# A fused two-layer graph network with a mixture of experts: the dispatch's triangle product a step later for full chunks, the router's product behind the second values for the first 16 batches

## The chip, the cores and the metric

The kernel runs on one core of one Trainium2 chip. Its time is device time in microseconds (us), as a median of several runs. A core has five engines that work in parallel, each with its own queue of instructions: TensorE (PE) for matmuls, VectorE (DVE) and ScalarE (ACT) for elementwise work, GpSimd (POOL), and SyncE (SP), which here only issues DMAs. POOL issues DMAs too, those that are addressed through a list of row numbers (indirect ones). In the profile PEld is TensorE's loading of weights, which runs beside its matmuls.

## The reference

The input `x` is 64 batches of 256 rows by 256 columns in float32, with one 256 x 256 adjacency matrix for all. Two layers follow each other, and each has an attention over the graph and a feed-forward part, both behind a layer norm and with a residual:

```python
x = x + _L0_gnn_ref(_layernorm(x), adj, L0_gnn_W, L0_gnn_a)        # 4 heads of 64, elu
x = x + _L0_ffn_ref(_layernorm(x), L0_ffn_weight, L0_ffn_bias)     # one linear
x = x + _L1_gnn_ref(_layernorm(x), adj, L1_gnn_W, L1_gnn_a)        # 1 head of 256, relu
x = x + _L1_ffn_ref(_layernorm(x), router_w, w1, b1, w2, b2)       # 8 experts, top 2

# the expert part, for tokens = the normed rows
probs = jax.nn.softmax(logits, axis=-1)
rw, re = jax.lax.top_k(probs, 2)
rw = rw / jnp.maximum(rw.sum(-1, keepdims=True), 1e-12)
out = tokens
for e in range(8):
    h = jax.nn.gelu(tokens @ w1[e] + b1[e], approximate=False)
    out = out + combine[:, e:e + 1] * (h @ w2[e] + b2[e])
```

`combine` holds a token's two weights at its two experts and zero elsewhere. Because `out` starts at the tokens, the last layer's output is the residual, plus the normed rows, plus what the experts add.

## The kernel before

Each batch's 256 rows are two tiles of 128 (NT = 2). `batch_layers` computes all of a batch up to its router logits. 62 batches then send each row to its two experts (dispatch), and the last two are computed with all experts (dense). The 62 go in chunks: 12 of four batches, six of two, two of one (`CHUNKS`). I call the 12 full chunks; in the code they are those with `spread`.

**How the order is made.** The whole order of work is written by the kernel itself. Each batch, each chunk's `route` and each expert pair is a Python generator, and the main loop (L1091 onwards) goes through time in steps. In a step every active generator is resumed once, in order of its rank, smallest first, and emits instructions until its next `yield r`, which sets its rank for the next step; a negative rank puts it back into the same step. Every engine gets its instructions in the order in which they are emitted. A batch takes three steps to the next (`TICKS`), so steps have phases 0, 1 and 2; a new batch begins in phase 2. `later(rank, *phases)` yields until a step of one of the phases comes. About five batches are under way at a time, each in another part of `batch_layers`.

**A batch.** The rows' mean and variance come from DVE (`norm_stats`: stats L374, mv L375), and POOL makes rstd of them (`finish_norms`: L382, L383). In most steps two norms meet, and one POOL pair of 128x4 serves both (`half_done` holds the first until the second comes). A norm that stays alone is finished at the end of the step, as 128x2. Then: layer 0's projections pq (L405), q scaled on DVE (L421), scores pd (L475) and z (L482), values pv (L496, 128x65), rinv (L503), the linear pf (L560) with x (L566, DVE, with rstd), layer 1's pq (L440), scores pd and z (L459, L464), values pv (L496, 128x257), their sum into x (L586), a last norm with `by` (L591, L594), the normed rows `xng` and the output's base (ACT, L600, L605), a transpose (pt L389, copied to xT by ACT, L395), and the router's product pl (L630), whose copy is the logits `lg` (L634). Of the ranks near the change: pl has 35, in phase 2, and the second values (pv 128x257) have 40, in the same step.

**A chunk's dispatch.** `route` begins in the step of its last pl. `top_two` gives one-hots of the two best experts and ends with their sum `m` (L948, all on DVE). Two products `pp` with a triangle of minus ones and with ones (PE, L956 and L957) count the rows of each expert; `both`, a running sum and a second addition (DVE, L959 to L975) make positions, `pos` (L978 to L985) picks each row's two, `ed` is an exponential on ACT (L961), `two_weights` (DVE, L679 to L682) makes the two weights, and the last copies (L989) put them beside the rows. In a full chunk these parts lie in steps of phase 2 (`m`), 0 (pp to L975), 2 (pos), 0 (weights, copies). Then POOL sends the rows (L922, an indirect DMA for each tile and expert, two a step, rank 95).

**Expert pairs.** A pair is 256 rows of one expert. SP loads its rows (xr, xt) once the chunk's sends have landed, DVE transposes them (sT), PE computes ph (L816) and py (L831), ACT the gelu between them (hT, L822), DVE adds the bias (y, L841), ACT multiplies by the weight (L809), and `scatter` (L852, rank 97, two indirect DMAs on POOL) adds the result to the output rows in DRAM. Pairs of different experts can meet in a row, so each scatter waits until those of the pair before it have landed.

In the last steps, the drain, no new batches come; norms then stay alone more often, and only pairs are left in the end.

Of the kernel before, what the change touches and what calls it, by code (L numbers as in the profile page):

```python
# [11 lines left out]
AF = mybir.ActivationFunctionType  # L12
# [15 lines left out]
def kernel(  # L28
# [17 lines left out]
    nc = tc.nc  # L46
# [5 lines left out]
    NT = N // P  # L52
# [307 lines left out]
    half_done = []  # L360
# [19 lines left out]
    def finish_norms(n):  # L380
        mv, rstd = half_done.pop()
        nc.gpsimd.tensor_scalar_add(rstd[:, :n], mv[:, :n, 1], EPS)  # L382
        nc.gpsimd.tensor_tensor(rstd[:, :n], rstd[:, :n], mhalf[:, :n], ALU.pow)  # L383

    def transposed(src, tag="xT", bufs=4, blocks=False):
        pt = bank("pt", [KT, N])
        for t in range(NT):
            for k in range(KT):
                nc.tensor.transpose(  # L389
                    pt[:, k, t * P : (t + 1) * P],  # L390
                    by_block(src[:, t, :])[:, k] if blocks else src[:, t, k * P : (k + 1) * P],
                    ident,
                )
        dst = work.tile([P, KT, N], F32, tag=tag, name="xT", bufs=bufs)
        nc.scalar.copy(dst, pt)  # L395
        return dst
# [109 lines left out]
    def batch_layers(b, c0, xng, lg):  # L506
# [23 lines left out]
        early = b < EARLY  # L530
# [92 lines left out]
            based.append(d.ins)  # L623
            nc.sync.nop()
        xT = transposed(xe[:, :, :D], *(("xTd", DENSE) if dense else ()), blocks=True)
        yield 35
        pl = bank("pl", [NT, E])
        for t in range(NT):
            for k in range(KT):
# [47 lines left out]
    def two_weights(less, second, ed):  # L677

        nc.vector.tensor_scalar(less, ed, 1.0, None, op0=ALU.add)  # L679
        nc.vector.reciprocal(less, less)  # L680
        nc.vector.tensor_tensor(second, ed, less, ALU.mult)
        nc.vector.tensor_tensor(less, less, second, ALU.subtract)  # L682
# [250 lines left out]
    def later(rank, *phases):  # L933

        yield rank
        while more and order_steps[-1] % TICKS not in phases:
            yield rank

    def route(c, row0, nt, n, last, xng, lg):

        rt = lambda shape, name, bufs=2, dt=F32: chunk_tile(shape, name, c, bufs, dt)
        vec, tt = nc.vector, nc.vector.tensor_tensor
        yield -90

        tail = rt([nt, 3], "tail")
        ohs, ed = top_two(c, nt, lg, tail[:, :, 0])
        m = rt([E, nt], "m")
        tt(m.rearrange("p e t -> p t e"), ohs[:, 0], ohs[:, 1], ALU.add)  # L948


        spread = nt == NTC
        yield from later(90, *((0,) if spread else (1, 2)))

        mf = m.rearrange("p e t -> p (e t)")
        pp = bank("pp", [2, E, nt])
        nc.tensor.matmul(pp[:, 0].rearrange("p e t -> p (e t)"), tri, mf, start=True, stop=True)  # L956
        nc.tensor.matmul(pp[:, 1].rearrange("p e t -> p (e t)"), ones, mf, start=True, stop=True)  # L957
        both = rt([2, E, nt], "both")
        vec.tensor_copy(both, pp)  # L959
        pre, tot = both[:, 0], both[:, 1]  # L960
        nc.scalar.activation(ed, ed, AF.Exp)  # L961
        tt(tot[:, :, 0], tot[:, :, 0], rows[0], ALU.add)
        run = rt([E, nt], "run")
        if nt == NTC:
            vec.tensor_tensor_scan(
                run.rearrange("p e t -> p (e t)"), scan_mask.rearrange("p e t -> p (e t)"),
                tot.rearrange("p e t -> p (e t)"), 0.0, ALU.mult, ALU.add,
            )
        else:
            for e in range(E):  # L970
                vec.tensor_tensor_scan(
                    run[:, e, :], ones[:, :nt], tot[:, e, :], 0.0, ALU.mult, ALU.add
                )
        rows[0] = run[:, :, nt - 1]
        tt(pre, pre, run, ALU.add)  # L975
        if spread:
            yield from later(90, 2)
        tt(  # L978
            ohs, ohs, pre.rearrange("p e t -> p t e")[:, None].to_broadcast([P, 2, nt, E]),
            ALU.mult,  # L980
        )
        posf = rt([2, nt], "posf")
        vec.tensor_reduce(posf, ohs, AX.X, ALU.add)
        pos = rt([2, nt], "pos", 4, I32)
        vec.tensor_copy(pos, posf)  # L985
        yield from later(90, *((0,) if spread else (1, 2)))
        two_weights(tail[:, :, 1], tail[:, :, 2], ed)
        for i, xe in enumerate(xng):
            vec.tensor_copy(xe[:, :, D + 1 :], tail[:, i * NT : (i + 1) * NT, :])  # L989
        parts = allot(c, n, False)  # L990
        if n and not spread:
            next(parts)
            ids, ef = next(parts)
        if last:
            ends_at = rt([E], "ends_at", 2, I32)
            vec.tensor_copy(ends_at, rows[0])
        yield 95
        mark = len(sent)
        for t in range(nt):
            for k in range(2):  # L1000
                send(xng[t // NT][:, t % NT, :], pos[:, k, t : t + 1])
            if n and spread and t in (1, 4):
                ids, ef = next(parts) or (None, None)
            if not last:
                yield 95
            elif t % 2:
                yield 95
        needs = sent[mark:]
        if n:
            regs = {}  # L1010
            waiting.extend(
                lambda j=j: expert_pair(j, n, ids, ef, regs, needs) for j in range(n)
            )
        if last:
            parts = allot(c + 1, FLUSH, True)
            next(parts)
            ids2, ef2 = next(parts)
            _, ends_sp = nc.values_load_multi_w_load_instructions(
                ends_at[0:1, :], engines=[mybir.EngineType.SP], min_val=0,
                max_val=(E * CAP - 1) * PAIR, skip_runtime_bounds_check_because="rows of a region",  # L1020
            )
            filled = []
            for e in range(E):
                d = nc.sync.dma_start(
                    out=xs_d[bass.ds(ends_sp[e], PAIR), :].rearrange("(p t) c -> p t c", t=2),
                    in_=fill,
                )
                tc.declare_no_dep(
                    d.ins, query=SYNC, group="rows", reason="filling rows lie behind an expert's last row"
                )  # L1030
                tc.add_to_no_dep_group("rows", d.ins)
                filled.append(d.ins.name)
                nc.sync.nop()
            yield 95
            regs2 = {}
            waiting.extend(
                lambda j=j: expert_pair(j, FLUSH, ids2, ef2, regs2, filled)
                for j in range(FLUSH)
            )
# [50 lines left out]
    with tc.manual_schedule():  # L1090
        while more or active or waiting or dense_jobs or scatters:  # L1091
            phase = step % TICKS
            if phase == 2 and more:
                nxt = next(batches, None)
                more = nxt is not None
                if more:
                    begin(nxt, 25)
            if step >= SETUP_AT and setup:
                begin(setup.pop(0)(), 90)
            if step >= QUIET:  # L1100
                if waiting and len(scatters) < 3:
                    begin(waiting.pop(0)(), 90)
            elif phase == 1:
                credit = min(credit + 3.0, 2.0 if step < DRAIN_AT else 3.0)
                while waiting and credit >= 1.0:
                    credit -= 1.0
                    begin(waiting.pop(0)(), 90)
            if dense_jobs and step % DENSE == 0:
                begin(dense_jobs.pop(0)(), 90)
            if scatters:  # L1110
                def one():
                    scatter()
                    return
                    yield
                begin(one(), 97)
            order_steps.append(step)
            queue = [(a[0], a[1], a) for a in active]
            heapq.heapify(queue)
            while queue:
                *_, entry = heapq.heappop(queue)  # L1120
                entry[0] = next(entry[2], None)
                if entry[0] is not None and entry[0] < 0:
                    entry[0] = -entry[0]
                    heapq.heappush(queue, (entry[0], entry[1], entry))
            if half_done:
                finish_norms(NT)
            active[:] = [a for a in active if a[0] is not None]
            step += 1
# [35 lines left out]
```

The softmax here doesn't subtract the row's maximum and nothing guards it: scores larger than these inputs give would overflow.

## Time and profile before

| what | value |
|---|---|
| median of 3 runs | 1607.51 us (1606.32 to 1608.09) |
| profiled execution | 1611.36 us, of which 1609.5 us is the span of the profile |
| PE busy | 1468.2 us (91%) |
| PE weight loads busy | 1299.9 us (81%) |
| DVE busy | 1308.6 us (81%) |
| POOL busy | 914.6 us (57%) |
| ACT busy | 860.2 us (53%) |
| mean granted PE clock | 0.963 |
| rows L831 py and L816 ph, PE | 266.5 and 243.6 us |
| row L496 pv, PE | 370.3 us |
| row L852 scatter, POOL | 417.0 us, 262 of 1592 ns |
| row L922 send, POOL | 251.2 us, 248 of 1013 ns |

The span in 40 equal slices of about 40 us, each digit the busy share in tenths, PEclk the clock that was granted to PE:

```profile
PE   7998988999999999999999999999999999489960
DVE  6898988999898989898989899899899987545530
POOL 2332636265757576666657575756665567733444
PEclk9999998999999999999999999999999999799985
```

The setup and the first batches fill the first slices. From the ninth slice on PE is full to within a tenth. In the 35th the last batches leave the pipeline, and after the 38th PE has next to nothing to do. A busy PE is not PE at its peak: matmuls are pipelined and their ends are modelled.

### The profile page before, as it was taken

How to read it: one execution, taken by the hardware profiler on the slowest of the kernel's cores; microseconds unless marked ns; L12 is line 12 of the kernel's file. 1: busy time of each engine (PE TensorE's matmuls, PEld its weight loads, DVE VectorE, ACT ScalarE, POOL GpSimd, SP SyncE). 2: the span in 40 equal slices, each digit the busy share in tenths (PEclk: the TensorE clock that was granted, in tenths of full speed). 3: DMA queues.
4: the chain of work that ended last, by engine and by line, in shares of the span. 5: the costliest groups of instructions: out<-in, count | busy, mean ns of one | idle time of the engine just before them, and what ended most of it. 6: DMA issues, size and time to landing. Idle time of an engine off the chain costs nothing.

```text
span 1609.5 us, 30304 instructions
## 1 busy us (share of the span) xinstructions
PE 1468.2 (91%) x8474; PEld 1299.9 (81%) x8474; DVE 1308.6 (81%) x4431; ACT 860.2 (53%) x1968; POOL 914.6 (57%) x875
## 2 busy tenths in 40 slices
PE   7998988999999999999999999999999999489960
PEld 5887777888888888888888888888888887468850
DVE  6898988999898989898989899899899987545530
ACT  2455455465666666556666665555556655343320
POOL 2332636265757576666657575756665567733444
PEclk9999998999999999999999999999999999799985
DMA  5712223466666666665657576664766566787733
GB/s 156 207 50 57 83 74 90 113 152 131 134 145 135 141 143 133 149 145 126 156 119 152 130 155 126 159 129 108 155 129 152 131 120 134 185 174 152 133 47 45
DMA packets 364134, 207.39 MB, mean 129 GB/s; under 512 B 264248, under 2 KB 334912, under 8 KB 363968
## 3 DMA queue, kind: packets, MB, share of 16 engines
q1 hardware_dynamic: 313344, 137.07, 34.7%
q0 software_dynamic: 49632, 67.39, 23.0%
q8 instruction: 70, 1.15, 0.3%
q10 hardware_dynamic: 992, 0.99, 0.2%
q14 instruction: 96, 0.79, 0.2%
HBM read 116.19 MB, written 89.15 MB: 128 GB/s over the span
## 4 chain that ended last, share of the span: by engine, by line
PE 70%; DVE 17%; DMA 3%; ACT 3%; issue 3%; POOL 2%; SPq 1%; DVEq 0%; POOLq 0%; ACTq 0%
PE pv L496 16%; PE ph L816 14%; PE py L831 14%; PE pq L405 6%; PE pq L440 6%; PE pf L560 5%; PE pt L389 4%; DVE z L482 3%; DVE stats L374 2%; PE pl L630 2%; ACT xT L395 2%; DMA out_dram<-y,xt 2%; POOL out_dram L852 1%; DVE mv L375 1%; PE pd L475 1%
## 5 line engine op out<-in xcount | busy, mean ns | idle before, releaser
L852 POOL DMA_INDIRECT out_dram<-y,xt x262 | 417.0, 1592 | 199.7 <-issue 51.1
L496 PE MATMUL pv<-q,z 128*128 128x65 f32 (+1 forms) x2560 | 370.3, 300 | 1.3 <-DVE z L482 1.3
L496 PEld LDWEIGHTS pv<-q,z 128*128 128x128 f32 x2560 | 331.5, 194 | 13.8 <-DVE z L482 1.4
L922 POOL DMA_INDIRECT xs<-xng,pos x248 | 251.2, 1013 | 66.4 <-issue 63.7
L382 POOL TENSOR_SCALAR rstd<-mv 128x4 f32<-128x4 f32 (+1 forms) x132 | 59.3, 449 | 395.5 <-DVE mv L375 347.5
L831 PE MATMUL py<-w2s,hT 128*128 (+1 forms) x1176 | 266.5, 380 | 1.2 <-ACT hT L822 1.2
L395 ACT COPY xT<-pt 128x512 f32<-128x512 f32 x192 | 113.7, 592 | 276.3 <-PE pt L389 276.3
L816 PE MATMUL ph<-sT,we 128*128 128x256 f32 x1048 | 243.6, 386 | 10.0 <-DMA we<-wpack 7.8
L831 PEld LDWEIGHTS py<-w2s,hT 128*128 128x128 f32 x1176 | 219.9, 191 | 30.0 <-ACT hT L822 2.0
L816 PEld LDWEIGHTS ph<-sT,we 128*128 128x128 f32 x1048 | 199.2, 194 | 37.2 <-issue 8.2
L482 DVE SCALAR_TENSOR_TENSOR z<-pd,q,mask 128x256 f32<-128x256 f32 x512 | 211.1, 474 | 0.9 <-PE pd L475 0.9
L822 ACT ACTIVATE hT<-ph,we 128x256 f32<-128x256 f32 x294 | 122.4, 472 | 152.9 <-PE ph L816 130.9
L383 POOL TENSOR_TENSOR rstd<-rstd,mhalf 128x4 f32<-128x4 f32 (+1 forms) x132 | 162.7, 1233 | 11.0
L374 DVE BATCH_NORM_STATS2 stats<-x 128x6 f32<-128x256 f32 x384 | 156.2, 407 | 2.2
L809 ACT ACTIVATE y<-y,w 128x256 f32<-128x256 f32 x262 | 112.4, 501 | 76.0 <-DVE y L841 75.5
L440 PE MATMUL pq<-wx,xT 128*128 128x259 f32 x512 | 130.1, 397 | 18.6 <-ACT xT L395 14.9
L405 PE MATMUL pq<-wx,xT 128*128 128x268 f32 x512 | 133.9, 407 | 5.6 <-DVE xT L116 3.7
L841 DVE TENSOR_TENSOR y<-py,b2s 128x512 f32<-128x512 f32 x131 | 85.9, 685 | 57.9 <-PE py L831 52.6
L440 PEld LDWEIGHTS pq<-wx,xT 128*128 128x128 f32 x512 | 92.5, 190 | 45.2 <-ACT xT L395 29.7
L560 PE MATMUL pf<-wfT,xT 128*128 128x256 f32 x512 | 122.8, 383 | 0.1
L405 PEld LDWEIGHTS pq<-wx,xT 128*128 128x128 f32 x512 | 99.0, 198 | 25.1 <-issue 3.2
L375 DVE BATCH_NORM_AGGREGATE mv<-stats 128x2 f32<-128x6 f32 x512 | 93.1, 182 | 17.5
(156 smaller groups left out, 2262.3 us busy)
## 6 DMA issues: line engine op xcount, KB each, us to landing
we<-wpack SPq DMA_DIRECT2D x139, 288.0 KB
xr<-xs SPq DMA_DIRECT2D x524, 64.0 KB
xblk<-in_x_dram SPq DMA_DIRECT2D x256, 64.0 KB
xin<-in_x_dram SPq DMA_DIRECT2D x64, 256.0 KB
out_dram<-base SPq DMA_DIRECT2D x64, 256.0 KB
out_dram<-y,xt POOLq DMA_INDIRECT x262, 4.1
xs<-xng,pos POOLq DMA_INDIRECT x248, 2.7
xs<-fill SPq DMA_DIRECT2D x9, 260.0 KB
```

The costliest lines, as they stand in the source:

```text
L374: nc.vector.bn_stats(stats[:, t, :], src[:, t, :])
L383: nc.gpsimd.tensor_tensor(rstd[:, :n], rstd[:, :n], mhalf[:, :n], ALU.pow)
L395: nc.scalar.copy(dst, pt)
L405: nc.tensor.matmul(pq.rearrange("p h c -> p (h c)"), xT[:, k, t * P : (t + 1) * P], wx[:, k, :], start=(k == 0), stop=(k == KT - 1),)
L440: nc.tensor.matmul(pq, xT[:, k, t * P : (t + 1) * P], wx1[:, k, :], start=(k == 0), stop=(k == KT - 1),)
L482: nc.vector.scalar_tensor_tensor(z[:, j, :], pd[:, i, :], q[:, j, h, d + 2 : d + 3], mask[:, j, :], op0=ALU.max, op1=ALU.mult,)
L496: nc.tensor.matmul(pv[:, h, :], z[:, j, t * P : (t + 1) * P], q[:, j, h, : d + 1], start=(j == 0), stop=(j == NT - 1),)
L560: nc.tensor.matmul(pf[:, t, :], xT[:, k, t * P : (t + 1) * P], wfT[:, k, :], start=(k == 0), stop=(k == KT - 1),)
L816: nc.tensor.matmul(ph[:, f, :], we[:, k * D + f * P : k * D + (f + 1) * P], xT[:, k, :], start=(k == 0), stop=(k == KT - 1),)
L831: nc.tensor.matmul(py[:, t, :], hT[:, f, t * P : (t + 1) * P], w2s[:, e, f * D : (f + 1) * D].rearrange("p e c -> p (e c)"), start=(f == 0 ...
L852: d = nc.gpsimd.indirect_dma_start(out=out_rows, out_offset=bass.IndirectOffsetOnAxis(ap=xt[:, t, 0:1].bitcast(I32), axis=0), in_=y[:, t, ...
L922: d = nc.gpsimd.indirect_dma_start(out=xs_d[: E * CAP * PAIR, :], out_offset=bass.IndirectOffsetOnAxis(ap=at, axis=0), in_=xe, in_offset=None,
```

## The change

Four things are edited.

- `batch_layers`: for the first 16 batches (`early`) the router's product pl gets rank 45 instead of 35, which puts it behind the second values (rank 40) in the same step.
- `route`, full chunks: the products pp, with the exponential of `ed`, move from the step of phase 0, rank 90, to that of phase 1, rank 45. The DVE work on them (both, the running sum, the addition) and `two_weights` follow in the step after, of phase 2, and pos with the last copies in the one after that, of phase 0. The sends stay in the step where they were.
- `route`, the eight smaller chunks: the steps of pp, pos and the copies stay; `two_weights` comes in the step of pp, in front of pos, instead of in the step of the copies.
- The main loop: before an entry of a rank above 75 is resumed, a norm that is still alone is finished, so its two POOL instructions stand ahead of that step's sends and scatters. Before, they stood at the end of the step.

```diff
--- before.py
+++ after.py
@@ -623,7 +623,7 @@
             based.append(d.ins)
             nc.sync.nop()
         xT = transposed(xe[:, :, :D], *(("xTd", DENSE) if dense else ()), blocks=True)
-        yield 35
+        yield 45 if early else 35
         pl = bank("pl", [NT, E])
         for t in range(NT):
             for k in range(KT):
@@ -949,16 +949,21 @@
 
 
         spread = nt == NTC
-        yield from later(90, *((0,) if spread else (1, 2)))
+        if spread:
+            yield from later(45, 1)
+        else:
+            yield from later(90, 1, 2)
 
         mf = m.rearrange("p e t -> p (e t)")
         pp = bank("pp", [2, E, nt])
         nc.tensor.matmul(pp[:, 0].rearrange("p e t -> p (e t)"), tri, mf, start=True, stop=True)
         nc.tensor.matmul(pp[:, 1].rearrange("p e t -> p (e t)"), ones, mf, start=True, stop=True)
+        nc.scalar.activation(ed, ed, AF.Exp)
+        if spread:
+            yield 90
         both = rt([2, E, nt], "both")
         vec.tensor_copy(both, pp)
         pre, tot = both[:, 0], both[:, 1]
-        nc.scalar.activation(ed, ed, AF.Exp)
         tt(tot[:, :, 0], tot[:, :, 0], rows[0], ALU.add)
         run = rt([E, nt], "run")
         if nt == NTC:
@@ -973,8 +978,9 @@
                 )
         rows[0] = run[:, :, nt - 1]
         tt(pre, pre, run, ALU.add)
+        two_weights(tail[:, :, 1], tail[:, :, 2], ed)
         if spread:
-            yield from later(90, 2)
+            yield 90
         tt(
             ohs, ohs, pre.rearrange("p e t -> p t e")[:, None].to_broadcast([P, 2, nt, E]),
             ALU.mult,
@@ -983,8 +989,8 @@
         vec.tensor_reduce(posf, ohs, AX.X, ALU.add)
         pos = rt([2, nt], "pos", 4, I32)
         vec.tensor_copy(pos, posf)
-        yield from later(90, *((0,) if spread else (1, 2)))
-        two_weights(tail[:, :, 1], tail[:, :, 2], ed)
+        if not spread:
+            yield from later(90, 1, 2)
         for i, xe in enumerate(xng):
             vec.tensor_copy(xe[:, :, D + 1 :], tail[:, i * NT : (i + 1) * NT, :])
         parts = allot(c, n, False)
@@ -1118,6 +1124,8 @@
             heapq.heapify(queue)
             while queue:
                 *_, entry = heapq.heappop(queue)
+                if half_done and entry[0] > 75:
+                    finish_norms(NT)
                 entry[0] = next(entry[2], None)
                 if entry[0] is not None and entry[0] < 0:
                     entry[0] = -entry[0]
```

No instruction is added or taken away. In the instruction order of the two kernels POOL's differs in four places, all in the drain, and SP's in none.

## Prediction

> **What bounds the kernel now.** I read the windows by stage first, then PE's and DVE's waits, then the timelines where a wait stood, and the chain of waits for the end. Every window starts with its stretch and length, then the busy time of PE, PEld, DVE, ACT and POOL, PE's granted clock, DMA share and GB/s:
>
> ```profile
> 145.00:200.00 55.00, 49.87 (x312) 43.67 (x311) 50.59 (x165) 27.36 (x80) 28.88 (x33) 0.97 0.24 73
> 330.00:700.00 370.00, 365.71 (x2191) 327.24 (x2190) 333.17 (x1101) 224.28 (x487) 244.28 (x228) 1.00 0.65 141
> 1310.00:1415.00 105.00, 80.55 (x393) 69.06 (x392) 69.98 (x325) 53.76 (x113) 73.61 (x68) 0.87 0.71 152
> 1550.00:1609.00 59.00, 4.06 (x19) 3.23 (x17) 1.38 (x2) 3.25 (x8) 25.50 (x17) 0.58 0.36 44
> ```
>
> There are three regimes. Up to about 314 us PE and DVE are equally full (49.87 and 50.59 of 55). From 330 to about 1284 PE is full (365.71 of 370). In the drain no engine is full, and after 1550 only POOL's scatters are left. PE's waits over the whole run:
>
> ```profile
> PE pp L956 <- DVE m L948: 19.8, 4, 11.3
> PE pl L630 <- ACT xT L395: 8.2, 7, 2.3
> PE pt L389 <- ACT xng L600: 8.0, 1, 8.0
> ```
>
> The four pp waits are 2.74 us at 134.91, 3.72 at 206.03, 2.05 at 281.22 and 11.26 at 1378.36. The first three (8.5 together) are full chunks in the early regime; the fourth is a small chunk in the drain. DVE in the drain:
>
> ```profile
> DVE by L591 <- POOL rstd L383: 18.1, 3, 10.1
> DVE x L566 <- POOL rstd L383: 9.0, 2, 6.4
> ```
>
> So the drain's long waits all come from rstd, made on POOL. POOL's timeline shows why (start, duration, work):
>
> ```profile
> 1337.75 1.02 POOL L922 DMA_INDIRECT xs<-xng,pos  x1 [0.18 <-issue]
> 1339.07 1.00 POOL L922 DMA_INDIRECT xs<-xng,pos  x1 [0.30 <-issue]
> 1340.42 1.61 POOL L852 DMA_INDIRECT out_dram<-y,xt  x1 [0.35 <-issue]
> 1342.34 1.57 POOL L852 DMA_INDIRECT out_dram<-y,xt  x1 [0.30 <-ACT hT L822]
> 1343.38 0.82 POOL L382 TENSOR_SCALAR rstd<-mv 128x2 f32<-128x2 f32 x1
> 1344.28 0.73 POOL L383 TENSOR_TENSOR rstd<-rstd,mhalf 128x2 f32<-128x2 f32 x1
> ```
>
> and DVE's on both sides of it:
>
> ```profile
> 1329.20 0.18 DVE L375 BATCH_NORM_AGGREGATE mv<-stats 128x2 f32<-128x6 f32 x1
> ...
> 1338.49 0.18 DVE L375 BATCH_NORM_AGGREGATE mv<-stats 128x2 f32<-128x6 f32 x1
> 1345.05 0.88 DVE L566 SCALAR_TENSOR_TENSOR x<-pf,rstd,x1b 128x256 f32<-128x256 f32 x2 [6.38 <-POOL rstd L383]
> ```
>
> The mv that this rstd reads was finished at 1329.38; the rstd stood behind two sends and a scatter pair, and DVE idled 6.38 us. The end itself is a chain of scatters (chain of waits):
>
> ```profile
> 1560.30 1.54 POOL out_dram L852
> 1561.84 0.30 issue
> 1562.14 3.77 DMA out_dram<-y,xt
> 1566.04 0.71 issue
> 1566.75 1.54 POOL out_dram L852
> ```
>
> A pair of scatters starts about 0.84 us after the pair before it has landed, at least 6.45 us a pair. I number the 131 pairs from 0. From pair 88 (1284.35) to pair 130 (1599.71) nearly all start so; what they lose beyond 0.84 us in the drain is POOL's norms and sends between two pairs: pair 93 4.71, pair 96 0.84, pair 100 2.26, pair 102 0.89, pair 103 1.52, and little else. y never holds them: the last y (ACT L809) is done at 1555.4, its scatter starts at 1599.7; pair 108's y is done by 1426.6 and goes at 1445.1. So only what moves this chain in the drain, or its start by way of PE, moves the end.
>
> **What the Trainium skill says.** "Perfetto Trace Analysis", Tensor Engine Instruction: ACT, DVE and GpSimd queues are strict FIFO, PE alone pulls weight loads ahead. The trace agrees: an rstd with its data ready since 1329.38 stood until 1343.38. "DMA: Bandwidth & Descriptors", Rules for kernel authors: an accumulating DMA needs the earlier DMA's semaphore before it touches the same bytes; that is the chain above, 0.84 us after each landing. "TensorE: Matmul & The Clock Gate", What's actually happening: after an idle window of about 3.4 us PE drops to half clock. The trace agrees: after the wait of 3.72 us eight pq matmuls (L405) took 3.89 us, where such a group takes 1.97 at full clock.
>
> **The change part by part.** No instruction is added or removed; PE, DVE, ACT and POOL only have theirs in another order. SP's order is the same, and POOL's differs in four places.
>
> *1. pp a step later for the 12 full chunks.* The one-hots (top_two and m, about 3.1 us of DVE) end at 205.88 in the second chunk; the products then stood in front of PE's pq at 206.03. Now PE meets them a step later, with m long ready: the three early waits go. But DVE was busy through them and does the same work after. What DVE loses to PE there is little: rinv waits 1.60 at 142.85 and 1.60 at 214.83, z (L464) 0.82 at 211.33. These go. In return both, add, scan, add (0.26+0.17+0.29+0.22, about 1.0 with gaps) leave the step where they filled DVE's wait for the norm chain (mv, POOL 1.34, ACT 0.44); in steps without them q (L421) waits 1.0 to 1.1. Chunk by chunk: -1.6+1.1, -1.6-0.8+1.1, and 0+1.0 for the third: -0.8. Bounds: all of DVE's early waits on PE (3.5 rinv, 0.8 z, 0.5 x between 100 and 314 us) gone and no new one, -4.8; no gain and three new waits, +3.3. At 313.8 PE takes over, waiting 1.82 for by, so DVE's time is what carries. I take -0.8.
>
> *2. pl behind pv for 16 batches.* PE's 7.9 us of early waits for xT lie where DVE sets the pace; pv comes earlier by pl's 0.96 us, lg (L634) later by pv's 1.98, and top_two follows on a DVE that is behind. 0; it lies within the bounds of part 1.
>
> *3. The nine full chunks after 330 us.* PE does the same work and is full, its waits there 16 us in all, none of them pp. both, add, scan, add and two_weights (1.0+0.75) come into phase 2 where pos (0.85) was: +0.9 us of DVE at that step's end, as much less in others. The same place takes the 3.1 us of top_two a batch earlier without PE waiting, so 0.9 is covered: 0. Uncovered it would be 12 x 0.9 = +10.8. The bank of pp is held one step longer, its next use lies 16 allocations on: 0. In the eight small chunks two_weights precedes pos: z 0.75 us later, under 24 ph matmuls (5.2 us): 0. Exp of ed moves by a step or less on an ACT that is 53% busy; its table loads stay 106: 0.
>
> *4. A single rstd ahead of everything of rank above 75.* On POOL this moves four norms, all in the drain: ahead of the sends and pair 92, of the sends and pair 95, of the sends and pair 99, and from behind pair 102 to before it. A single norm costs 1.0 alone and 1.6 behind a scatter. Queued behind it are two sends (1.3 each) and the pair.
> - Pair 92: the norm's mv is ready (1310.25), the sends start 1.1 later; the pair +1.0. Its rstd is there at 1313.6, so x (L566) is bound by its own place on DVE, 1317.4 instead of 1319.97; the pair norm that follows and was waited for (mv at 1321.92) runs 2.6 earlier; pair 93 -2.7 and pair 94 -2.8 (1331.1).
> - Pair 95: IOTA, norm, two sends from 1334.0: 1338.8, -1.6. Its rstd is done at 1336.0, and L566 now starts when DVE is through its earlier work, 1338.67+0.75 = 1339.4, not 1345.05. The next pair norm is done by 1343.7; pair 96 is bound by landing, 1346.1: -2.5. Pairs 97 and 98 keep this.
> - Pair 99: norm and sends end at 1367.5, landing asks for 1367.8: -2.5. by (L591) comes at about 1365 instead of 1374.85. Pair 100: four sends without the norm (1.8) before them, 1376.8: -3.4. Pair 101 the same.
> - Pair 102: POOL had 4.67 idle in front of it, so the norm is free there: -3.4. Pair 103: four sends, no norm: 1400.6, against 1404.99: -4.4.
>
> From pair 104 on landing bounds every pair, and 26 of them keep the -4.4. PE's 11.3 and 8.0 us of waiting shrink too, beside the chain. Bounds of part 4: each norm delays its pair and nothing is regained, about +2; all loss beyond 0.84 us gone (4.71+0.84+2.26+0.89+1.52), about -10.2.
>
> Sum: -0.8 + 0 + 0 - 4.4 = -5.2. The profiled execution has a span of 1609.5 and took 1611.36, 1.9 around the span: 1604.3 and 1606.2 after. It lies 3.85 above the median of the three runs (1607.51); the same -5.2 on that gives 1602.3.
>
> **The rivals.**
> - *A, the early idle time carries too.* If the pp waits drag DVE along, part 1 gives its bound: 1607.5-4.8-4.4 = 1598.3. For: PE's clock is down in 200-215 us (0.77). Against: DVE is 50.59 of 55 busy.
> - *B, the drain gives nothing.* The earlier rstd moves loads and PE work beside the scatters, whose own flights run from 2.2 to 5.5 us after issue, and the 4.4 is lost to them: 1607.5-0.8 = 1606.7. For: flights were over 4 us at pairs 102, 103 and 105. Against: the loads still wait for the same sends.
> - *C, slower: phase 2 of the full chunks.* both to two_weights at the end of that step delay the next step's x, z and q by 0.9 us; if DVE is not 0.9 ahead of PE's need there, each of 12 chunks pays: +10.8-5.2 = +5.6, 1613.1. It decides from about 0.4 us a chunk (5.2 over 12). For: DVE is 90% busy in 330-700. Against: top_two in the same place.
> - *D, it does not do what it says*: pp's wait turns up at the next PE instruction. Then part 1 is 0 and the time 1603.1; inside the forecast.
>
> **How the numbers follow.** A measurement of this kernel can tell about 0.2%, 3.2 us, from no change: faster is below 1604.3, slower above 1610.7. Forecast 0.45 (own range 1599 to 1606; 0.36 of it faster, 0.09 same), A 0.15 (faster), B 0.23 (0.02 faster, 0.19 same, 0.02 slower), C 0.17 (slower by 0.16, same 0.01). Sums: faster 0.53, same 0.29, slower 0.18. The range runs from A's 1598 to 1611, short of C.
>
> **What would show it.** Right: no pp wait over 0.5 us before 314; x L566 and by L591 waiting for rstd under 8 us in all, from 27.1; pair 103 near 1399.8 (-5.2); the spacing after it unchanged; PE's sum for 330-700 the same. Wrong: PE waits on DVE in full chunks after 330 (C), pair 103 early but the spacing behind it longer (B), or PE-bound from well before 314 (A).

## The result and the profile after

The changed kernel took 1610.78 us (median of 22 runs, 1603.19 to 1615.25), the kernel before 1606.92 us in as many runs beside it. The ratio is 1.0024, with a 95% interval of 1.0013 to 1.0035: slower, by about 4 us, where 5.2 us less were forecast. The profiled execution took 1611.09 us with a span of 1609.3, which is close to its median; the one of before (1611.36) lay 4.4 above its own, so the two profiles, with nearly equal spans, hide the difference. It has to be looked for by stage.

The windows of the changed kernel (stretch, length, busy PE, PEld, DVE, ACT, POOL, clock, DMA share, GB/s):

```profile
145.00:200.00 55.00, 50.81 (x288) 43.53 (x289) 49.80 (x165) 26.77 (x79) 29.10 (x32) 0.92 0.24 73
330.00:700.00 370.00, 365.94 (x2193) 327.70 (x2192) 332.58 (x1099) 223.53 (x485) 243.49 (x227) 1.00 0.65 140
1310.00:1415.00 105.00, 81.54 (x406) 70.88 (x404) 70.85 (x330) 54.17 (x112) 74.52 (x69) 0.87 0.71 153
1550.00:1609.00 59.00, 3.71 (x18) 2.92 (x16) 1.38 (x2) 2.91 (x7) 25.52 (x17) 0.55 0.36 44
```

In 145 to 200 us PE makes 24 matmuls fewer (288, not 312) in more busy time, at a clock of 0.92 instead of 0.97. The full stretch is as it was. PE's waits from 100 to 314 us:

```profile
PE pp L959 <- DVE m L948: 5.6, 3, 2.6
PE pl L630 <- ACT xT L395: 1.7, 3, 0.8
```

pl's waits went, from 7.9 us, but pp still waits for m in each of the first three chunks. In the third chunk PE's timeline reads (start, duration, work, and in brackets the idle time before it and its releaser):

```profile
280.46 0.43 PE L959 MATMUL pp<-m,tri 128*128 128x64 f32 x2 [2.56 <-DVE m L948]
280.73 0.39 PE L960 MATMUL pp<-m,ones 128*128 128x64 f32 x2
280.95 5.31 PE L496 MATMUL pv<-q,z 128*128 128x65 f32 x32
286.06 1.06 PE L389 MATMUL pt<-ident,xng 128*128 128x128 f32 x4
286.91 3.25 PE L560 MATMUL pf<-wfT,xT 128*128 128x256 f32 x8
```

In the kernel before, where pp stands in front of pq, the same pv took 3.68 us and pf 1.89:

```profile
281.22 0.41 PE L956 MATMUL pp<-m,tri 128*128 128x64 f32 x2 [2.05 <-DVE m L948]
...
281.69 2.03 PE L405 MATMUL pq<-wx,xT 128*128 128x268 f32 x8
...
283.77 3.68 PE L496 MATMUL pv<-q,z 128*128 128x65 f32 x32
...
287.80 1.89 PE L560 MATMUL pf<-wfT,xT 128*128 128x256 f32 x8
```

DVE now waits for what they make:

```profile
290.20 0.88 DVE L566 SCALAR_TENSOR_TENSOR x<-pf,rstd,x1b 128x256 f32<-128x256 f32 x2 [0.80 <-PE pf L560]
```

In the drain POOL's order changed as described; the norm now stands in front of the sends and pair 95:

```profile
1337.18 0.89 POOL L382 TENSOR_SCALAR rstd<-mv 128x2 f32<-128x2 f32 x1
1338.16 0.73 POOL L383 TENSOR_TENSOR rstd<-rstd,mhalf 128x2 f32<-128x2 f32 x1
1339.08 1.09 POOL L922 DMA_INDIRECT xs<-xng,pos  x1 [0.20 <-issue]
1340.48 1.00 POOL L922 DMA_INDIRECT xs<-xng,pos  x1 [0.30 <-issue]
1341.78 1.61 POOL L852 DMA_INDIRECT out_dram<-y,xt  x1 [0.30 <-issue]
```

and x no longer waits for it (6.38 us before):

```profile
1339.13 0.86 DVE L566 SCALAR_TENSOR_TENSOR x<-pf,rstd,x1b 128x256 f32<-128x256 f32 x2
```

DVE's waits for rstd from 1290 to 1420 us are 13.0 us (by, four times), from 27.1. The chain of waits at the end is the old one, a pair each 6.4 us:

```profile
1560.18 1.54 POOL out_dram L852
1561.72 0.30 issue
1562.02 3.73 DMA out_dram<-y,xt
1565.88 0.71 issue
1566.59 1.54 POOL out_dram L852
```

### The profile page after: what moved, and what is told of

Read it like the earlier page. It is cut to its first block, busy times and chain, and to the rows that moved or that the text cites. A ratio compares the mean times of both kernels' runs of the same rounds, so it can differ in the third digit from the quotient of the medians.

```text
span 1609.3 us, 30296 instructions
## 1 busy us (share of the span) xinstructions
PE 1470.2 (91%) x8474; PEld 1301.5 (81%) x8474; DVE 1305.8 (81%) x4431; ACT 860.0 (53%) x1968; POOL 914.8 (57%) x875
## 5 line engine op out<-in xcount | busy, mean ns | idle before, releaser
L405 PE MATMUL pq<-wx,xT 128*128 128x268 f32 x512 | 130.8, 399 | 5.7 <-DVE xT L116 3.6
L560 PE MATMUL pf<-wfT,xT 128*128 128x256 f32 x512 | 127.1, 393 | 0.1
L405 PEld LDWEIGHTS pq<-wx,xT 128*128 128x128 f32 x512 | 97.9, 194 | 26.0 <-issue 3.7
```

The source lines that it names most:

```text
L405: nc.tensor.matmul(pq.rearrange("p h c -> p (h c)"), xT[:, k, t * P : (t + 1) * P], wx[:, k, :], start=(k == 0), stop=(k == KT - 1),)
L560: nc.tensor.matmul(pf[:, t, :], xT[:, k, t * P : (t + 1) * P], wfT[:, k, :], start=(k == 0), stop=(k == KT - 1),)
```

## The experiments

All ratios are to the kernel before in runs on the same chip, with 95% intervals. To place a loss I use DVE's sum into x (L586), one a batch: its start in a trace minus that in the first trace of before. Starts differ by up to 4 us from the first batches on, in all kernels and by chance, so what counts is the change from batch 4 to batch 17.

**The three edits one by one, and before again.** The first theory was that the moved pp in the early chunks cost the time.

norm_only, the main loop's edit on the kernel before:

```diff
                 *_, entry = heapq.heappop(queue)
+                if half_done and entry[0] > 75:
+                    finish_norms(NT)
```

> The kernel before with the main loop's edit alone (a single rstd ahead of ranks above 75). Theory T1 (the loss sits in the early chunks, where the moved pp products stand in front of pv 128x65): the edit is the only part that gains, as predicted for the drain, -1 to -4 us against before; pair 103 starts 1.5 to 5 us earlier. Theory T2 (the drain loses: norms ahead of the sends hold sends and scatters, and their flights get longer): +2 to +4 us, all of the loss of the whole change. Theory T3 (no one part, the end is set by the flights of the scatters, which differ from run to run): within 1 us.

pl_only, on the kernel before:

```diff
-        yield 35
+        yield 45 if early else 35
```

> The kernel before with the router's product behind the second values for the first 16 batches alone. T1: -1 to 0 us, since batches 6 to 8 began 0.75 to 1.0 us earlier in the changed kernel's trace, before any chunk was dispatched. T2 and T3: within 1 us. If it loses (+1 or more), lg comes too late for top_two, which T1 does not expect.

route_only has the edits in `route` and neither of these two; their core:

```diff
-        yield from later(90, *((0,) if spread else (1, 2)))
+        if spread:
+            yield from later(45, 1)
+        else:
+            yield from later(90, 1, 2)
...
+        if spread:
+            yield 90
         both = rt([2, E, nt], "both")
```

> The kernel before with the edits in route alone (pp in phase 1 in full chunks, two_weights earlier in all). T1: +2 to +5 us, with PE's pp waits for m still there in the first chunks (5 to 6 us in all), pv 128x65 behind them at a lower clock, and batch 20 about 2 us later than before. T2: within 1 us. T3: within 1 us.

> The kernel before once more, for a second trace of it, since its first profiled run (1611.36) lay 4.4 us above the median of its 22 runs (1606.92). T3: the same starts up to pair 91 within 0.3 us and another end, by the flights of the scatters alone. T1 and T2 expect that the early batches start within 0.3 us of the first trace too; if they do not, the early stretch itself varies from run to run.

| kernel | ratio | L586 from batch 4 to 17, us |
|---|---|---|
| norm_only | 0.9982 [0.9969, 0.9995] | +2.0 |
| pl_only | 1.0053 [1.0032, 1.0075] | +4.6 |
| route_only | 0.9986 [0.9976, 0.9997] | -1.8 |
| before_again | 1.0006 [0.9990, 1.0022] | -0.4 |
| changed kernel | 1.0024 [1.0013, 1.0035] | +1.5 |

The changed kernel is not behind from the start: at batch 9 it is 3.0 us ahead of the first trace. It loses 2.1 us from batch 9 to 10 and 1.9 from 13 to 14, behind the pp of the second and the third chunk, where pv took 5.43 and 5.31 us.

The theory fell at once: route gains. Its PE waits from 60 to 330 us (of the kernel before: pp 8.5 in three, pl 8.2 in seven) are

```profile
PE pl L630 <- ACT xT L395: 12.5, 9, 2.5
...
PE pp L959 <- DVE m L948: 0.7, 1, 0.7
```

so PE still waits, but in these pieces of 2.5 us at most. What loses, 8.5 us, is pl's edit, which was costed at nothing. The trace of pl_only shows where. The largest piece, 2.9 us from batch 12 to 13, lies behind the pp of its third chunk. Others are 1.1 us from batch 7 to 8 and 2.1 from 14 to 16, where the clock is down from 170.5 and from 317.3 us, and from batch 4 to 5 it gains 1.8, because a drop that the kernel before has at 136 us is missing. PE in the third chunk:

```profile
281.37 0.66 PE L956 MATMUL pp<-m,tri 128*128 128x64 f32 x2 [4.68 <-DVE ohs L668]
281.82 0.63 PE L957 MATMUL pp<-m,ones 128*128 128x64 f32 x2
282.25 3.89 PE L405 MATMUL pq<-wx,xT 128*128 128x268 f32 x8
285.93 0.63 PE L459 MATMUL pd<-ident,ex 128*128 128x128 f32 x2
```

and DVE behind it:

```profile
286.67 0.88 DVE L464 SCALAR_TENSOR_TENSOR z<-pd,ex,me 128x256 f32<-128x256 f32 x2 [0.79 <-ACT q L413]
290.18 0.18 DVE L503 RECIPROCAL rinv<-pv 128x4 f32<-128x4 f32 x1 [1.60 <-PE pv L496]
```

In the kernel before, as its lines above show, the wait in front of this pp was 2.05 us and pq took 2.03; DVE did not wait. m itself is finished at 281.22 here and at 281.07 there, so DVE was on time up to this point; the L586 that follows starts at 290.92 instead of 288.23, so some 2.5 us are lost behind m. That suggested the clock: PE is ahead of DVE in this stretch and has to wait somewhere. Its waits of over 0.3 us from 130 to 320 us add up to 18.0 us before and to 18.4 in pl_only. The waits in front of pl broke them into smaller pieces; without these PE runs on to pp and takes more in one.

**Is it the clock?** pl_warm keeps PE busy through the wait. The 12 matmuls are extra work without a reader:

```diff
+        if c < 3:
+            warm = bank("warm", [D])
+            for _ in range(12):
+                nc.tensor.matmul(warm, ident, wfT[:, 0, :], start=True, stop=True)
         mf = m.rearrange("p e t -> p (e t)")
```

> pl_only, and PE makes 12 matmuls of 128x256 into a bank that nobody reads (2.6 us) in front of pp in the first three chunks, where pl_only waits 3.3, 5.4 and 4.7 us for m; they are extra work whose result is left out. Theory C (the loss is the clock: PE's waits are gathered into one of over 3.4 us, the clock drops to half and DVE then waits for pv, pd and pf): the pq matmuls after pp take about 2.0 us instead of 3.9, and most of the 4.4 us lost by batch 16 comes back, 3 to 6 us less than pl_only. Rival L (the loss is that lg and with it top_two and m come later on DVE): nothing comes back, m and batch 16 stand where pl_only has them or 0 to 2 us later.

The ratio is 0.9985 [0.9973, 0.9997]: 0.0068, 11 us, off pl_only, by adding work. From batch 4 to 17 it gains 2.4 us where pl_only loses 4.6. PE in the third chunk:

```profile
273.56 5.35 PE L957 MATMUL warm<-wfT,ident 128*128 128x256 f32 x24
279.00 0.43 PE L960 MATMUL pp<-m,tri 128*128 128x64 f32 x2
279.27 0.39 PE L961 MATMUL pp<-m,ones 128*128 128x64 f32 x2
279.49 2.02 PE L405 MATMUL pq<-wx,xT 128*128 128x268 f32 x8
```

The filling was twice as long as I had reckoned (each float32 matmul is two in the trace: 24, 5.35 us), and in the first chunk it holds pp 1.8 us past m; it gains all the same. pq is at 2.02. The windows from 278 to 293 us, of the kernel before, of pl_only and of pl_warm, show the clock (last but two: 1.00, 0.77, 1.00):

```profile
278.00:293.00 15.00, 12.95 (x90) 11.73 (x89) 14.19 (x48) 6.09 (x16) 4.80 (x8) 1.00 0.39 92
```

```profile
278.00:293.00 15.00, 11.63 (x64) 10.39 (x65) 11.89 (x42) 4.83 (x12) 3.75 (x6) 0.77 0.46 108
```

```profile
278.00:293.00 15.00, 14.67 (x97) 13.00 (x96) 14.38 (x47) 3.13 (x8) 3.99 (x6) 1.00 0.53 130
```

DVE, the bound there, is busy 14.38 of 15 us instead of 11.89. The rival, a later lg, is out as the main cause: pl_warm has the same late lg.

The filling does more than undo the edit. From batch 4 to 17 PE is at half clock for 23.9 us in the first trace of before, for 30.7 in pl_only and for 3.4 in pl_warm, so the 11 us are not the price of pl's edit alone. The means over all runs go the same way: the granted clock is 0.9633 before, 0.9604 in pl_only, 0.9616 in the changed kernel and 0.9677 in pl_warm. A filled kernel without pl's edit, which would separate the two, was not run.

**The edits taken out of the changed kernel one by one.** no_pl, no_norm and no_route are the changed kernel, each without the edit of its name.

> The changed kernel with the router's product back at its old place (its other edits kept). So far pl_only stands at 1.0053 against before, route_only at 0.9986 and norm_only at 0.9982. Theory P (the router's product behind the second values is the whole loss, the other two edits each gain 2 to 3 us): 0.996 to 0.998, 1601 to 1604 us. Rival S (the gains of the other two overlap or come from run-to-run differences of the start and the drain): 0.998 to 1.000.

> The changed kernel without the main loop's edit. P: pl +8.5 and route -2.2 add up to +6.3, about 1.004, 1613 us. If route takes away what pl costs (pp no longer stands in front of pq, so PE's wait is shorter and its clock stays), less: 1.002. S: 1.002 to 1.0025, the changed kernel's own ratio.

> The changed kernel without the edits in route. P: pl +8.5 and norm -2.9: +5.6, about 1.0035, 1612 us. If the wait of pp is what makes pl cost (it was 3.3, 5.4 and 4.7 us with pl alone), the early loss is that of pl_only: batch 20 about 4.5 us later than before at the same start.

| kernel | ratio | L586 from batch 4 to 17, us |
|---|---|---|
| no_pl | 0.9986 [0.9972, 0.9999] | -2.2 |
| no_norm | 1.0015 [1.0000, 1.0031] | +1.8 |
| no_route | 1.0034 [1.0022, 1.0046] | +6.4 |

Without pl's edit the change is a gain. Each edit can now be priced in four pairs of kernels that differ in it alone; pairs with and without pl (pl_only and before, no_route and norm_only, no_norm and route_only, the changed kernel and no_pl) give +0.53, +0.52, +0.29 and +0.38%, mean 0.43%, 6.9 us. The traces of these pairs show 4.6, 4.4, 3.7 and 3.7 us of it between batch 4 and 17; where the rest lies is not shown. route gives -0.14, +0.04, -0.38 and -0.10%, mean 2.3 us of gain, most where pl is in: it puts pq and pd in front of pp, so the wait there is shorter. norm gives -0.18, 0.00, -0.19 and +0.09%, mean 1.1 us of gain. A single pair is uncertain by about 0.2%, so the last mean is not clear of nothing, and route's only just.

**Which of the 16 moves?** pl_last moves the product in batches 3, 7, 11 and 15 alone, pl_others in the other twelve:

```diff
-        yield 35
+        yield 45 if early and b % 4 == 3 else 35
```

> The kernel before, with the router's product behind the second values only in batches 3, 7, 11 and 15, the last of each early chunk. Theory C (PE, no longer held at pl, runs on to pp and waits there in one piece, over 3.4 us, and its clock drops): these four moves carry the loss of pl_only, 1.003 to 1.006, with pp waits of 4 us and more. Rival G (all 16 moves matter, each by a little): about a quarter, 1.001.

> The kernel before, with the product moved in the other 12 of the first 16 batches. C: within 0.001 of before, since pp's wait in front of it is as before (2 to 3.8 us). G: about three quarters of the loss of pl_only, 1.004.

pl_last 1.0016 [1.0000, 1.0032], pl_others 1.0021 [1.0008, 1.0033]. Neither theory fits: the four moves do not carry all of the 0.53%, and the twelve carry less than three quarters of it. The third chunk, of pl_last and then of pl_others, shows why either half will do:

```profile
281.89 0.66 PE L956 MATMUL pp<-m,tri 128*128 128x64 f32 x2 [5.36 <-DVE ohs L668]
...
282.78 3.84 PE L405 MATMUL pq<-wx,xT 128*128 128x268 f32 x8
```

```profile
274.67 0.66 PE L956 MATMUL pp<-m,tri 128*128 128x64 f32 x2 [3.67 <-DVE m L948]
...
275.55 3.89 PE L405 MATMUL pq<-wx,xT 128*128 128x268 f32 x8
```

Both stretch the wait in front of pp, to 5.36 and 3.67 us from 2.05, and both drop the clock. From batch 4 to 17 they lose 3.5 and 2.6 us. How long the clock is down does not tell the loss by itself: in pl_last it is 20.5 us between these batches, less than in the first trace of before, so it counts where it falls. Theory C fails as it was stated: the long wait in front of pp does not come from the last batch's move alone.

**A better version.** after_warm is the changed kernel with six of the filling matmuls (`range(6)`), norm_pl_warm is no_route with twelve.

> The changed kernel with 6 matmuls of 128x256 into a bank that nobody reads in front of pp in the first three chunks; they are extra work, 2.7 us of PE each time by the 12 that took 5.35 us in pl_warm. C: pv behind pp takes 3.7 us instead of 5.3 and the kernel comes to 0.996 to 0.999 of before. If pl costs the changed kernel in another way than by the clock, 1.001 to 1.003.

> pl_warm with the main loop's edit: 0.996 to 0.998 if the two gains add up (0.9985 and 0.9982 alone), the candidate for the fastest; 0.9985 if the norm's gain in the drain is lost again in the flights of the scatters.

after_warm comes to 0.9983 [0.9968, 0.9998], norm_pl_warm to 0.9984 [0.9974, 0.9994]. In after_warm pv behind pp is at full clock again:

```profile
276.42 0.41 PE L963 MATMUL pp<-m,tri 128*128 128x64 f32 x2
276.66 0.39 PE L964 MATMUL pp<-m,ones 128*128 128x64 f32 x2
276.88 3.74 PE L496 MATMUL pv<-q,z 128*128 128x65 f32 x32
```

With the waits filled the changed kernel is as fast as no_pl (0.9983 and 0.9986): what pl's edit costs it comes back, and that points to the clock once more, with the reservation made for pl_warm. No version gained more than 0.2%; norm_only, route_only, no_pl, pl_warm and these two can't be told apart.

## Why the prediction was wrong

**The step that failed is part 2**, pl behind pv: "0; it lies within the bounds of part 1". It measured +6.9 us. The reasoning was that PE's waits for xT lie where DVE sets the pace. That is right, and DVE's own work hardly moved: m of the third chunk was 0.15 us later in pl_only. What I left out is that an idle PE is not free of consequence. The sum of PE's waits stayed (18.0 and 18.4 us), but the order decides their pieces, and behind the new ones PE ran at half clock where DVE needed its results: in the third chunk pq took 3.89 us instead of 2.03. "TensorE: Matmul & The Clock Gate" of the Trainium skill, What's actually happening, which I had cited, says that an idle window of about 3.4 us throttles PE. I used it only to explain a slow pq of before, and did not ask what the edit does to the waits. The trace of before held more than that: after the wait of 2.74 us at 134.91, well under 3.4, pq took 3.17 us.

Part 1, pp in phase 1, was right in sign and roughly in size: -0.8 forecast; in the traces of the two kernels with route's edit and without pl's, -1.8 and -2.2 by batch 17 and -1.0 and -1.2 by batch 20; by the two pairs without pl's edit, which are not clear of nothing, -0.8. But my picture of it was wrong: pp does not find m "long ready". On PE it moved behind pq and pd only, 2.1 us, and "no pp wait over 0.5 us before 314" failed with 5.6 us. In route_only, where that wait is 0.7 us, pl's waits are 12.5 us instead: the idle time went there, in pieces of at most 2.5. That is rival D, the wait that turns up elsewhere on PE; it priced this at nothing.

Part 3, nothing in the full stretch: right. From batch 20 to 55 each batch's first pq (L405) starts between 0.65 and 1.12 us later in the changed kernel than in the first trace of before, with no drift. Rival C is out.

Part 4, the norms in the drain: the norms did go ahead and the chain did start sooner, but the size is half or less. Over eight traces without the edit and six with it, pair 103 starts 96.3 and 94.5 us after pair 91: 1.8 us sooner, not 4.4. Two terms were mis-sized. Pair 93 starts 1.7 us sooner in the mean instead of 2.7, and, to judge by the start of pair 94, it lands some 4.1 us after its issue instead of 2.9; pair 94 keeps 0.4 of the 2.8 I gave it. Then pair 95, with the norm in front of it, starts 0.6 us later instead of 1.6 sooner. DVE's waits for rstd came to 13.0 us, where I had asked for less than 8. In the changed kernel's trace pair 93 took 4.88 us to land, and POOL stood 3.14 us in front of pair 94:

```profile
1324.89 1.61 POOL L852 DMA_INDIRECT out_dram<-y,xt  x1 [0.30 <-issue]
...
1334.11 1.60 POOL L852 DMA_INDIRECT out_dram<-y,xt  x1 [3.14 <-ACT y L809]
```

That is rival B for this part, at a price of some 2.6 us. That pair 93 lands later because it now meets the loads of rows and weights is argued from their places, not shown. Of the rivals, A expected the freed waits of PE to make DVE faster by up to 4.8 us, and less came. C, the way to a slower kernel, sought the cost in the full stretch; no rival had a lower clock in the early one.

## What to carry to other kernels

Where PE runs ahead of the engine that sets the pace, its idle time is not free: an edit that costs nothing by the sum of the waits can gather them into other pieces, as from 2.05 us to 4.68 here, and the engine that was the bound then waits for a PE at half clock. So read the granted clock and the time of the matmuls behind each PE wait, before and after. Filling such a wait with matmuls that nobody reads is a cheap test of that, and here a remedy; to price one edit by it, the kernel without the edit has to be filled too. A chain of transfers started sooner may land more slowly in its new place, so a gain on it is to be sized with the flights of that place.

## What the runs showed of the hardware

The drop of the clock is not decided by the wait's length alone. After waits of 2.05, 2.40 and 2.02 us in front of the third pp, before and in two kernels that are the same in this stretch, pq took 2.03, 2.03 and 2.75; after 3.33 us in the first chunk it took 2.02 in pl_only and 3.89 in no_route. From 3.67 us on it was never at full clock (2.79 to 3.89). Shorter waits can be enough: after 1.98 and 2.56 us the changed kernel's pv took 5.43 and 5.31, and in pl_only the clock is 0.50 from 170.6 to 177 us, behind a wait of 0.98. In all the traces the stretches of half clock last 3.4 us or a multiple of it (but for the last of each, which the end cuts off). This fits the free-running window of about 3.4 us that the same section of "TensorE: Matmul & The Clock Gate" describes; but where that section has a whole window idle before the drop, here much less idle time was followed by one. It makes some 2 us of early time a matter of chance: norm_only, with the early order of before, lost 2.0 us there.

Medians of this kernel came with single runs that lay 7 to 14 us apart. One source stands in twelve of the fourteen traces, all but the first of before and that of the changed kernel, at 1138 to 1150 us: PE's pv group falls apart, and nothing that the profile shows holds it. In before_again:

```profile
1143.16 0.22 PE L496 MATMUL pv<-q,z 128*128 128x65 f32 x1 [0.50 <-issue]
1143.88 0.31 PE L496 MATMUL pv<-q,z 128*128 128x65 f32 x1 [0.50 <-issue]
1145.31 0.42 PE L496 MATMUL pv<-q,z 128*128 128x65 f32 x2 [1.11 <-issue]
```

From the first pq of batch 57 to that of batch 58 it took 28.8 us, where the first trace of before took 24.0, without this. What holds the issue there was not tried.
